# Two mixture layers that multiply only the chosen experts, with their steps placed inside the attentions

## The chip, the core and the metric

The kernel runs on one core of a Trainium2 chip. The metric is device time in microseconds (us), from one launch on that core. TensorE is called PE below, VectorE DVE, ScalarE ACT, GpSimd POOL, and SP is the engine that issues most DMAs.

## The reference

The program is a stack of four layers on `x` of shape 16 x 112 x 256 (16 batches of 112 tokens, 256 channels, float32), with a context of 16 x 375 x 256. Each layer does

```
x = x + tanh(g_xattn[l]) * attention_l(layernorm(x), ctx)
x = x + tanh(g_ffn[l])   * ffn_l(layernorm(x))
```

Attentions 0, 1 and 2 have 16 heads of width 16; attention 1 also has a mask and a clip; attention 3 has one head. The second halves are: layers 0 and 1 a mixture of 8 experts (256 to 256 channels each) of which every token uses the best two, weighted by its gates; layer 2 a set of 8 experts with fixed token blocks and a GELU; layer 3 a gated unit with FP4 quantisation. What the change touches is this:

```
gates    = softmax(x @ gate_w.T + gate_b)                # 8 per token
top2     = top_k(gates, 2)                               # layer 1: top_k of the logits, then softmax
out      = sum over the 2 chosen e of gate_e * (x @ expert_w[e] + expert_b[e])
```

## The kernel before

Tokens are handled in 4 groups of 4 batches (`G = 4`, 448 tokens). All of `x` and all of the transposed context stay in SBUF. The four compute engines run in the order in which the program emits their instructions (a manual schedule); SP's order is left to the scheduler.

The layers run one after the other. `attention(pool, layer, w)` goes over the batches b = 0..15 in a hand-written order which is software-pipelined: scores of batch b+1 and b+2 are made while batch b is weighted. In the unmasked form (layers 0 and 2) one batch on PE is: `exponentials` (L449, L461) three times, `maxima` (scores L398, whose maximum DVE takes at L414) four times, `both_keys` (L203), `values_of` (L365), `weighted` (L485) three times, `max_rows` (L434) and `output` (L522). The maxima go through POOL (`max_parts`, L422 and L425) before `max_rows`. In the masked form (layer 1) a batch is four units of four heads; a unit is scores (L398), a clip and a maximum on DVE (L548, L565), a minimum on POOL (L567), the exponential on ACT (L570), transposes (L582) and the weighting (L599). The layernorm of the next group is spread over the units of its first batch, and its last part puts three small operations, four normalisations (L269) and four additions of the output bias (L273) on POOL in one go. `one_over` (L614) on POOL and `one_over_T` (L622) on PE follow once a batch.

PSUM has two pools: three tiles of two banks each (`wide`), for scores and exponentials, and two single banks (`bank`). One of the two single banks holds the weighted sums `po` of a batch from its first `weighted` to `normalised` in the next batch, so one is left for keys, values, outputs and maxima in turn.

A mixture is a stage of its own. `Mixture.rest` goes over 16 batches, and for each of them `experts` multiplies the 112 tokens by all 8 experts, whose weights were loaded to SBUF as one tile of 2 MB. Every chosen or unchosen product is added to `x` on DVE with its gate, which is zero for the six that were not chosen:

```
for q in range(2):
    pe = wide(f"pe_{nm}_{q}")
    for n in range(2):
        c0 = (2 * q + n) * 512
        for k in range(2):
            nc.tensor.matmul(pe[:S, n, :], xT[:, k, j * S : (j + 1) * S],          # L871
                             self.ew[:, k, c0 : c0 + 512], start=(k == 0), stop=(k == 1))
    for i in range(4):
        nc.vector.scalar_tensor_tensor(xb, pe[...], gt[:, j, e : e + 1], xb, ...)   # L881
```

Between them lie, once a group, the layernorm (POOL), eight transposes (L187), the gate logits (L823) and the choice of the best two on DVE. Nothing of the next attention can start before the mixture of its first group is done, and its first steps (keys, values and queries of batch 0) follow the last mixture batch.

## Time and profile before

| what | us |
|---|---|
| median of 3 runs (1704.04 to 1705.53) | 1704.33 |
| the profiled execution | 1703.84 |
| its span, first to last instruction | 1701.6 |
| attention 0, to the last output product on PE | 0 to 323 |
| mixture 0, first transpose L187 to the keys of attention 1 | 324.1 to 471.4 |
| attention 1 (masked) | 471.4 to 868 |
| mixture 1 | 868.2 to 1014.9 |
| attention 2 | 1014.9 to 1329 |
| fixed-block experts, then layer 3 | 1329 to 1701.6 |

The times of the stages are read from the timeline of PE. A PE matrix product of float32 operands is recorded as two instructions, a transpose as one. The share of a wait is shown with what ended it; a stage in which PE is busy nearly all the time is one in which PE's work sets the time.

### The profile page before, as it was taken

The page shows a single profiled execution, that of the slowest core. Times are in us where ns is not written, and L with a number is a line of the kernel's source. Part 1 is how long each engine was busy: PE and PEld are TensorE (multiplying, and loading weights), DVE is VectorE, ACT ScalarE, POOL GpSimd, SP SyncE. Part 2 cuts the span into 40 slices and gives each one's busy share as a digit, 9 for nine tenths or more (in the row PEclk, how much of TensorE's full clock was granted, in tenths as well). Part 3 has the DMA queues.
Part 4 walks back from the last instruction along what each step waited for, and adds up shares of the span by engine and source line. Part 5 has one row for each costly group of instructions (what it writes and reads, how often), then busy time and mean ns, then how long its engine had stood idle before and what let it go on. Part 6 is the DMA issues. An engine that isn't in the chain of part 4 may idle for free.

```text
span 1701.6 us, 31829 instructions
## 1 busy us (share of the span) xinstructions
PE 1585.0 (93%) x13228; PEld 1008.9 (59%) x13228; DVE 1055.8 (62%) x1925; ACT 715.2 (42%) x1439; POOL 417.2 (25%) x856
## 2 busy tenths in 40 slices
PE   7999999999988989899899999999999899999997
PEld 3666665644456656566554444666666788666765
DVE  3565666766676766767846654565666434377775
ACT  2444444300056766677720003444444433455532
POOL 2202010212123232423310110231212334333342
PEclk8999999999999999999979998999999999999999
DMA  9000000000010000000000010000000542100000
GB/s 277 8 2 2 2 8 8 25 7 4 1 54 9 6 8 9 9 12 9 18 7 1 0 25 11 1 2 2 8 2 17 168 148 98 33 12 21 17 11 17
DMA packets 21410, 45.81 MB, mean 27 GB/s; under 512 B 4139, under 2 KB 16827, under 8 KB 18875
## 3 DMA queue, kind: packets, MB, share of 16 engines
q1 hardware_dynamic: 20835, 43.79, 8.4%
q8 instruction: 104, 1.70, 0.4%
q14 instruction: 39, 0.32, 0.1%
q10 hardware_dynamic: 432, 0.01, 0.0%
HBM read 41.95 MB, written 1.84 MB: 26 GB/s over the span
## 4 chain that ended last, share of the span: by engine, by line
PE 80%; DVE 7%; ACT 7%; POOL 4%; issue 2%; DMA 0%; SPq 0%; POOLq 0%; ACTq 0%; DVEq 0%
PE pe_m L871 13%; PE pv L365 8%; PE ps L398 8%; PE pk L203 7%; PE pe L582 6%; PE pt L449 6%; PE po L485 5%; PE py_f L966 3%; PE py L522 3%; PE ph L950 3%; PE po L599 2%; PE pq L203 2%; PE pgu_h L1289 2%; PE py L1323 2%; PE pt L461 1%
## 5 line engine op out<-in xcount | busy, mean ns | idle before, releaser
L414 DVE TENSOR_REDUCE nm<-ps 112x2 f32<-112x750 f32 x256 | 228.3, 933 | 196.2 <-PE ps L398 196.2
L871 PE MATMUL pe_m<-w_L_ffn_expert_w,xT_m 128*112 128x512 f32 x512 | 233.9, 610 | 0.0
L398 PE MATMUL ps<-kT,qm 32*112 32x375 f32 x1536 | 195.3, 528 | 20.5 <-ACT kT L329 9.6
L470 ACT ACTIVATE ex<-pt 125x896 f32<-125x896 f32 x192 | 165.6, 915 | 72.9 <-PE pt L461 72.9
L881 DVE SCALAR_TENSOR_TENSOR x<-pe_m,gt_m,x 112x256 f32<-112x256 f32 x256 | 123.7, 483 | 83.9 <-PE pe_m L871 75.2
L871 PEld LDWEIGHTS pe_m<-w_L_ffn_expert_w,xT_m 128*112 128x112 f32 x512 | 90.4, 182 | 121.8 <-issue 120.9
L570 ACT ACTIVATE sm<-sm,nmax 112x375 f32<-112x375 f32 x256 | 152.3, 599 | 8.0 <-POOL nmax L567 7.0
L582 PEld LDWEIGHTS pe<-ident,sm 112*125 112x125 f32 x768 | 105.7, 196 | 80.6 <-ACT sm L570 69.4
L582 PE MATMUL pe<-ident,sm 112*125 112x112 f32 x768 | 126.2, 294 | 26.6 <-ACT sm L570 26.1
L548 DVE SCALAR_TENSOR_TENSOR sm<-ps,up 112x750 f32<-112x750 f32 x128 | 114.0, 932 | 53.0 <-PE ps L398 52.0
L398 PEld LDWEIGHTS ps<-kT,qm 32*112 32x112 f32 x1536 | 66.3, 173 | 93.5 <-issue 39.1
L565 DVE TENSOR_REDUCE nmax<-sm 112x2 f32<-112x750 f32 x128 | 112.9, 924 | 0.0
L449 PE MATMUL pt<-qm,kT 32*125 32x224 f32 x1536 | 109.1, 381 | 3.1 <-ACT qm L355 1.7
L365 PE MATMUL pv<-w_L_xattn_wv,ctx 128*125 128x256 f32 x384 | 104.8, 413 | 0.0
L485 PE MATMUL po<-ex,vpad 125*32 125x112 f32 x3072 | 94.2, 262 | 0.7 <-ACT ex L470 0.7
L203 PE MATMUL pk<-ctx,w_L_xattn_wk 128*128 128x375 f32 x256 | 94.2, 502 | 0.0
L485 PEld LDWEIGHTS po<-ex,vpad 125*32 125x32 f32 x3072 | 70.6, 109 | 38.8 <-issue 30.4
L386 POOL TENSOR_SCALAR oT<-oT,w_L_xattn_bv 128x112 f32<-128x112 f32 x64 | 35.6, 565 | 224.0 <-DVE oT L512 173.3
L449 PEld LDWEIGHTS pt<-qm,kT 32*125 32x125 f32 x1536 | 72.9, 186 | 27.1 <-issue 17.5
L365 PEld LDWEIGHTS pv<-w_L_xattn_wv,ctx 128*125 128x125 f32 x384 | 71.6, 199 | 21.7 <-DVE x L525 7.1
L1289 PE MATMUL pgu_h<-wT,fT_f 128*112 128x352 f32 x256 | 80.1, 467 | 0.7 <-DVE x L1334 0.5
L586 ACT COPY eT<-pe 125x672 f32<-125x672 f32 x96 | 68.2, 712 | 20.3 <-PE pe L582 17.7
(254 smaller groups left out, 2513.3 us busy)
## 6 DMA issues: line engine op xcount, KB each, us to landing
w<-in_L_ffn_w_dram SPq DMA_DIRECT2D x16, 1024.0 KB, 6.2
ctx<-in_ctx_dram SPq DMA_DIRECT2D x16, 375.0 KB, 8.6
w_L_ffn_expert_w<-in_L_ffn_expert_w_dram SPq DMA_DIRECT2D x2, 2048.0 KB, 8.0
mk<-in_mask_Bx1xSxS_ik_dram SPq DMA_DIRECT2D x16, 164.1 KB, 2.3
mask<-in_mask_BxSxS_ff_dram SPq DMA_DIRECT2D x16, 164.1 KB, 2.2
x<-in_x_dram SPq DMA_DIRECT2D x4, 448.0 KB, 9.6
out_dram<-x SPq DMA_DIRECT2D x16, 112.0 KB, 1.9
w_L_ffn_w_gate_up<-in_L_ffn_w_gate_up_dram SPq DMA_DIRECT2D x1, 1408.0 KB
```

The costliest lines, as they stand in the source:

```text
L203: nc.tensor.matmul(ps[:, :n], w[:, k, c * P : (c + 1) * P], rhs[:, k, :], start=(k == 0), stop=(k == 1))
L365: nc.tensor.matmul(pv[:TC, i * D : (i + 1) * D], rhs_of(b)[:, k, t * TC : (t + 1) * TC], w["wv"][:, k, :], start=(k == 0), stop=(k == 1),)
L398: nc.tensor.matmul(ps[:S, i, :T], qms[g][rows, c, p, j * S : (j + 1) * S], kTs[b][rows, c, :], start=True, stop=True,)
L414: nc.vector.tensor_reduce(nms[b][:, cp, 2 * h : 2 * h + 2], ps[:S, :, :T], AX.X, ALU.max, negate=True)
L449: nc.tensor.matmul(pairs[r // 2][:TC, r % 2, q * 2 * S : (q + 1) * 2 * S], kTs[b][rows, c, t * TC : (t + 1) * TC], qms[g][rows, c, :, j * ...
L470: nc.scalar.activation(e[:, 2 * h : 2 * h + 2].rearrange("t r q p s -> t r (q p s)"), pairs[h][:TC, :, : 4 * S], AF.Exp)
L485: nc.tensor.matmul(po[32 * r : 32 * r + 32, (2 * c + p) * S : (2 * c + p + 1) * S], vp[:, t, 4 * c + r, 2 * p : 2 * p + 2, :], e[:, r, q, ...
L570: nc.scalar.activation(sm[:, i, :], sm[:, i, :], AF.Exp, bias=nmax[:, i : i + 1], accum_out=rss[b][:, head : head + 1])
L582: nc.tensor.transpose(pt[:TC, i, t * S : (t + 1) * S], sm[:, 2 * h + i, t * TC : (t + 1) * TC], ident[:S, :S])
L871: nc.tensor.matmul(pe[:S, n, :], xT[:, k, j * S : (j + 1) * S], self.ew[:, k, c0 : c0 + 512], start=(k == 0), stop=(k == 1),)
L881: nc.vector.scalar_tensor_tensor(xb, pe[:S, i // 2, o0 : o0 + D], gt[:, j, e : e + 1], xb, ALU.mult, ALU.add)
L1289: nc.tensor.matmul(ps[:S, n, : FI // 2], fTs[u][:, 2 * k + i, :], wT[m][:, k, n * (FI // 2) : (n + 1) * (FI // 2)], start=(k == 0), stop=( ...
```

## The change

The stage of the mixture is gone. A mixture is now three lines of small steps, each written as a generator, which are taken in turn at fixed places of the attention code. `route` normalises a group, makes gates and the best two, counts for each token its place among the tokens of its expert (products with a triangular matrix), and scatters the normalised rows with indirect DMAs from POOL to a DRAM tensor in which each expert has a region of 512 rows. It also makes a table of 14 slots: which expert, and which first row. `products` goes over these 14 slots: SP reads expert and row from the table into registers, loads that expert's weights (256 KB), its bias (128 KB, broadcast) and 128 rows of the group (128 KB); PE transposes the rows and multiplies them; DVE adds the bias; SP stores 128 rows to a second DRAM tensor. `combine` gathers for each token its two rows by indirect DMA and adds them to `x` with their gates.

`fill()` takes one step of each of the three lines, which work on different groups at a time. In an unmasked batch it is called five times: F1 after the third `maxima`, F2 after `both_keys`, F3 after the second `weighted`, F4 after the last `maxima`, F5 after the last `weighted`. In a masked batch it is called after the scores of every unit (FA) and, in the second and fourth unit, once more after the weighting of the unit before (FB). Group g of a mixture is queued when its attention has finished it, so the third and fourth group of a mixture are worked on within the next attention.

```diff
+    def products(layer, g, routed):
...
+        def read(s):
+            e = nc.sync.value_load(table[0:1, s : s + 1], min_val=0, max_val=E - 1)
+            r = regs[s] = nc.sync.value_load(table[0:1, NS + s : NS + s + 1], min_val=0, max_val=ROWS - P)
+            w = moe.tile([P, 3 * D], F32, tag="w", name=f"w_{nm}_{s}")
+            nc.sync.dma_start(w[:, : 2 * D]..., a[L + "expert_w"][:, :, bass.ds(e * D, D)])
+            nc.sync.dma_start(w[:, 2 * D :], a[L + "expert_b"][bass.ds(e, 1), :].partition_broadcast(P))
+            xg = moe.tile([P, D], F32, tag="xg", name=f"xg_{nm}_{s}")
+            nc.sync.dma_start(xg, rows_in[g][bass.ds(r, P), :])
+            loaded[s] = w, xg
+
+        read(0)
+        yield
+        read(1)
+        yield
+        for s in range(-1, NS):
+            pt = bank(f"pm_{nm}_{s}")
+            if s + 1 < NS:
+                xg = loaded[s + 1][1]
+                for k in range(2):
+                    nc.tensor.transpose(pt[:, k * P : (k + 1) * P], xg[:, k * P : (k + 1) * P], ident)
+                xgT = turnedT[s + 1] = moe.tile([P, D], F32, tag="xgT", ...)
+                nc.scalar.copy(xgT, pt[:, :D])
+            if s >= 0:
+                w, xgT = loaded.pop(s)[0], turnedT.pop(s)
+                for k in range(2):
+                    nc.tensor.matmul(pt[:, D : 2 * D], xgT[...], w[...], ...)
+                y = moe.tile([P, D], F32, tag="y", name=f"y_{nm}_{s}")
+                nc.vector.tensor_tensor(y, pt[:, D : 2 * D], w[:, 2 * D :], ALU.add)
+                nc.sync.dma_start(rows_out[g][bass.ds(regs.pop(s), P), :], y)
+                read(s + 2)
+            yield
...
+        def copy_out(j):                      # in route: four of these, one a step
+            for i in range(2):
+                nc.gpsimd.indirect_dma_start(rows_in[g], ...index[:, i, j : j + 1]..., xn[:, j, :], None)
...
+        def gather(j):                        # in combine
+            yg = got[j] = moe.tile([S, 2, D], F32, tag="yg", name=f"yg_{nm}_{j}")
+            for i in range(2):
+                nc.gpsimd.indirect_dma_start(yg[:, i, :], None, rows_out[g], ...index[:, i, j : j + 1]...)
...
+    def fill():
+        for i, make in enumerate((route, products, combine)):
+            line = lines[i]
...
+            if next(job[3], "end") == "end":
+                line.popleft()                # and on to the next line
+        next(said.get("side", iter(())), None)
...
                 maxima(b + 1, 2)
+                fill()                        # F1
                 values_of(b + 1, (0, 1))()
...
                 both_keys(b + 2)
+                fill()                        # F2
                 maxima(b + 2, 0)
                 weighted(b, 1)
+                fill()                        # F3
...
                 maxima(b + 2, 1)
-                if at == 0:
-                    norm_part(g, 2)
-                    norm_part(g, 3)
+                fill()                        # F4
                 weighted(b, 2)
+                if at == 2:
+                    bias_part(g, range(G))
+                fill()                        # F5
...
                 masked_scores(*ahead)
+                fill()                        # FA
                 turned(b, cp, 0)
                 if u:
                     weighted_masked(*units[u - 1])
+                if cp % 2:
+                    fill()                    # FB
...
-                        self.experts(g, j)
```

The rows, weights and outputs of the slots have two buffers each. In the emitted order every indirect scatter waits for the one before it, and the stores of a group wait for one another, since they write one DRAM tensor. The two DRAM tensors of each kind are cleared once by SP, 5.1 MB each, during batches 0 to 3 of attention 0.

Around this, the parts of the layernorm are placed anew: in attention 1 the four normalisations come at the end of the third batch of a group and the bias additions in two halves in the fourth, and no longer in one go. The first steps of the next attention (keys and queries of its batch 0) move into the tail of the attention before. The quantisation of the last layer's down weights, done beside mixture 0 before, becomes side steps of `fill` in attention 0, in four smaller pieces.

## The prediction

> **What bounds the kernel now.** I read the page's busy shares and its chain first, then busy time by stretch, then the timeline of one batch.

> ```profile
> PE 1585.0 (93%) x13228; PEld 1008.9 (59%) x13228; DVE 1055.8 (62%) x1925; ACT 715.2 (42%) x1439; POOL 417.2 (25%) x856
> PE 80%; DVE 7%; ACT 7%; POOL 4%; issue 2%; DMA 0%; SPq 0%; POOLq 0%; ACTq 0%; DVEq 0%
> 23.00:313.00 290.00, 275.91 (x3433) 174.14 (x3436) 176.54 (x267) 125.83 (x194) 41.49 (x115) 0.98 0.08 24
> 328.00:471.00 143.00, 138.13 (x396) 59.90 (x396) 99.03 (x265) 8.37 (x19) 22.05 (x37) 0.98 0.01 3
> 482.00:866.00 384.00, 343.88 (x3234) 233.10 (x3234) 278.02 (x404) 258.46 (x688) 124.90 (x262) 0.95 0.03 10
> 871.00:1015.00 144.00, 139.53 (x397) 61.61 (x398) 89.88 (x250) 5.07 (x12) 20.52 (x37) 0.96 0.01 2
> ```

> The rows by stretch give length, then busy PE, PE weight load, DVE, ACT, POOL, then the granted clock, DMA share and GB/s. PE is busy for 95 to 97% of attention 0 and of both mixtures, and 90% of masked attention 1; DMA moves nothing there. So removed PE work pays in full, and PE work added to an attention costs in full, and so does every wait put into PE's queue. Here is PE in one unmasked batch (start, length, what):

> ```profile
> 104.87 1.04 PE L398 MATMUL ps<-kT,qm 32*112 32x375 f32 x8
> 105.84 2.79 PE L203 MATMUL pk<-ctx,w_wk 128*128 128x375 f32 x8
> 109.51 0.90 PE L398 MATMUL ps<-kT,qm 32*112 32x375 f32 x8 [0.87 <-ACT kT L329]
> 110.34 0.97 PE L485 MATMUL po<-ex,vpad 125*32 125x112 f32 x32
> 111.25 0.37 PE L434 MATMUL pm<-identb,mparts 112*128 112x112 bf16 x4
> 111.55 1.04 PE L449 MATMUL pt<-qm,kT 32*125 32x224 f32 x16
> 112.41 0.37 PE L461 MATMUL pt<-mr,onesb 3*125 3x224 bf16 x8
> 112.71 1.13 PE L365 MATMUL pv<-w_wv,ctx 128*125 128x256 f32 x4
> 113.77 0.95 PE L398 MATMUL ps<-kT,qm 32*112 32x375 f32 x8
> 114.65 0.97 PE L485 MATMUL po<-ex,vpad 125*32 125x112 f32 x32
> ```

> F2 stands at 108.6 (in the wait for kT), F3 at 111.25, F4 at 114.65, F5 at 115.55. The reader sees how close the places are: between F2 and F3 only 1.75 us of PE work (scores .85, weighting .9), F4 to F5 .9, F3 to F4 3.4, F5 to F1 3.0 (exponentials 1.2, output .9, scores .9), F1 to F2 7.7. In a masked batch the same reading gives 1.7 from FA to FB, about 3.3 from FB to the next FA, 5 or more where there is no FB.

> **What is removed.** Mixture 0 runs from 324.05 to 471.38 and mixture 1 from 868.18 to 1014.85: 147.3 + 146.7 = 294. Two `po`, two `py` and the twelve transposes of the down weights in them stay: 5. That leaves 289. DVE loses 124 us of L881; it bounds nothing here and I count it nowhere. The second gain is the layernorm in attention 1:

> ```profile
> 507.44 2.17 POOL xn_a L269 x4
> 507.78 0.78 PE L599 MATMUL po<-eT,vpad 125*32 125x112 f32 x24
> 509.58 2.76 POOL L273 TENSOR_TENSOR x<-x,grow_a 112x256 f32<-112x256 f32 x4
> 512.28 0.39 POOL L614 COPY rx<-ri 112x256 f32<-112x256 f32 x1
> 512.73 0.64 PE L622 MATMUL pr<-ident,rx 112*128 112x112 f32 x2 [4.17 <-POOL rx L614]
> 511.80:515.20 3.40, 2.47 (x10) 2.38 (x11) 0.00 (x0) 0.89 (x2) 1.28 (x4) 0.50 0.00 0
> ```

> PE waits 4.17 for a copy that stands behind 6.5 us of POOL work, and then runs at clock 0.50 for about 3.9 us, which costs another 1.95. This happens three times (508, 605, 704). The new order puts `rx` ahead of the normalisations and halves the additions: 3 x 6.1 = 18. Together 307.

> **PE work added.** A slot has two transposes of 128 (.13 each, from L187, 8 in 1.06) and two products of 256 wide (.48 each, L365 at 1.92 for four): 1.19. There are 14 slots x 4 groups x 2 layers = 112, so 133. Note that 14 x 128 = 1792 rows is half of the 3584 of before, not a quarter: padding eats the rest. Routing costs a group 1.06 transposes, 1.65 logits (L823) and about .8 for some 18 small products: 3.5 x 8 = 28. Steps that stand where PE waits anyway are free: FA precedes L582, which waits about .4 for ACT at 43 of them, -15.

> **The wait that the change adds.** This is the main term. Rows for slot s+2 are requested after `y` of slot s, and are transposed in the very next step. The request stands on SP behind the store of y(s), 256 KB of weights and 128 KB of bias. Landing times:

> ```profile
> mask<-in_mask_BxSxS_ff_dram SPq DMA_DIRECT2D x16, 164.1 KB, 2.2
> out_dram<-x SPq DMA_DIRECT2D x16, 112.0 KB, 1.9
> w_L_xattn_wq<-in_L_xattn_wq_dram SPq DMA_DIRECT2D x3, 256.0 KB, 2.5
> ```

> [...] Three DMAs go ahead of the rows, .42 to .45 apart (b to w at 1336.81 and 1337.23, plus an address computation): 1.35. Landing is 1.9 alone. The three rows fit 1.4 + 4.5 ns per KB, so the store, weights and bias ahead of it (512 KB, 2.3 us of data) push it to 2.9 at worst; I take 2.55. R = 4.6, bounds 4.0 and 5.1. PE, in order, waits R minus the gap: F2 to F3 2.85, F3 to F4 .9 (longer gap in the batch with queries), F4 to F5 3.7, F5 to F1 1.6, F1 to F2 none: 9.0 in five, 1.8 a step. Masked: 2 x 2.9 + 2 x 1.3 in six, 1.4 a step. Slots 0 and 1 of a group are read two steps ahead, so 96 waits count; by the emitted order 41 fall in unmasked batches, 55 in masked ones: 74 + 77 = 151 (at R = 4.0 110, at 5.1 184). Behind the waiting PE stand scores, so DVE, ACT and POOL idle too, and nothing gives it back.

> **Smaller waits.** With one free PSUM bank, `pv` after F1 and `pm` after F3 wait for y: .7 each, .25 a slot, 28; F2 fills the .87 for kT in ten batches, -9. Routing takes the bank six times a group and hands it on through ACT or DVE, about 1 us each: 48. Sum 67 (25 to 85).

> POOL: the scatters of a pair wait for each other. The trace has no indirect DMA; the nearest row is the .112 MB store, 1.9. [...]

> SP: 28 register reads a group, 26 of them ahead of the first rows, five steps (18 to 20 us) before PE wants these. No register read is in the trace. [...] I take 0, range 0 to 110; there is no gain in it.

> Mask loads come on the same SP queue, but are issued a unit ahead; hidden unless SP stalls. Clearing (20 MB at the 270 GB/s of the first 23 us: 76 us) runs beside batches 0 to 3: 0, with up to 10 if a piece of the down weights lands behind it. The moved first steps of attentions 1 and 2 cost the same PE time.

> **Clock.** The row at 511.8 shows 0.50 after a wait of 4.17. [...] By the trace shorter waits also pay: about 2.3 us of transposes and logits at 353.5 were followed by 0.59. With all 34 waits above 2.8 us, 66. I take 30 (0 to 66; below nothing is excluded, 1.00 being most of the time granted).

> **Sum.** 1701.6 - 307 + 133 + 28 - 15 + 151 + 67 + 16 + 30 = 1804.6, plus the 2.2 outside the span (1703.84 - 1701.6): 1807. The profiled execution lies 0.5 below the median of 1704.33, so nothing is to be converted. All low ends: 1678; all high ends: about 2060.

> **Rivals.** (1) *Faster: the reads land soon enough.* If R is 3.0, the waits fall to .67 and .43 a step, 51, and none trips the clock: 1701.6 - 307 + 133 + 28 - 15 + 51 + 67 + 16 = 1675, with the 2.2 1677. It decides in favour from about R = 3.5 downward. [...] For: smaller waits may be less than 67. [...] (3) *The change doesn't do what it says.* Halved, not quartered, rows: taken in above. If all waits vanished, 1701.6 - 307 + 146 + 2 = 1543 would be the end; nothing in the trace lets one expect that.

> **Numbers.** Forecast .57 (1740 to 1870), rival 1 .18, rival 2 .20, a balance near zero .05. What a measurement of this kernel can tell from no change is about 0.2%. Range 1680 to 1950: it leaves out the better half of rival 1 and the upper half of rival 2.

> **What would show it.** In the profile after: PE rows of the rows' transposes (`pm_m`) with waits of 1 to 4 us put down to the DMA `xg`, some 150 in all, longest at F5 and F3; PE's busy share falling below 90%; dips of the clock there; a pair of scatters of about 4 us on POOL; batches of about 34 us instead of 17.9 where products run. Waits for `xg` below 50 in all, or first slots waiting over 10 us, would make the prediction wrong.

## The result, and the profile after

The changed kernel takes 2225.27 us (median of 4 runs, 2218.96 to 2232.72) where the kernel before takes 1704.18 on the same chip: a ratio of 1.306, 95% interval 1.3014 to 1.3106. The profiled execution took 2228.51 us, its span 2226.8. "Slower" was right, and the wait that the rows put on PE was right in place and, partly by luck, in size, but the loss is 521 us where 103 were forecast, far outside the range. One term, the clock, was too small by a factor of eight, and one wait was not in the sum at all.

First the page after: busy shares, the rows of the 40 slices for PE and for its granted clock, and the chain that ended last.

```profile
PE 1733.4 (78%) x13404; PEld 1164.5 (52%) x13404; DVE 1011.9 (45%) x1965; ACT 754.3 (34%) x1550; POOL 546.8 (25%) x1003
PE   7898777677676766766766766777779999999998
PEclk7999786877867866786787677768679999999999
PE 39%; ACT 8%; DVE 7%; issue 5%; DMA 5%; POOL 3%; SPq 2%; POOLq 0%; DVEq 0%; ACTq 0%
```

PE's share falls from 93% to 78% and no other engine's share rises. PE is no longer the whole chain: 39% after 80%. From slice 5 to slice 30, which is where mixture steps stand, the busy digit is 6 or 7 and the clock digit mostly 6 to 8; from slice 31 on both are 9. So two things are lost together: time in which PE does nothing, and speed in the time in which it works. The same by stretch (length, busy PE, weight load, DVE, ACT, POOL, granted clock, DMA share, GB/s):

```profile
313.00:800.00 487.00, 346.76 (x2576) 228.14 (x2577) 193.48 (x411) 138.06 (x312) 109.66 (x183) 0.74 0.24 67
800.00:1300.00 500.00, 349.93 (x2207) 236.36 (x2207) 201.55 (x386) 166.93 (x446) 116.35 (x203) 0.74 0.21 61
1300.00:1715.00 415.00, 304.25 (x2533) 193.46 (x2532) 170.89 (x335) 121.86 (x248) 97.97 (x175) 0.78 0.21 59
1715.00:1820.00 105.00, 100.84 (x1311) 65.00 (x1312) 62.15 (x95) 49.19 (x79) 18.21 (x47) 1.00 0.01 4
```

In 313 to 1715 PE sits idle for 401 us. What it does in the rest, it does at 0.74 to 0.78: 346.76 x 0.26 + 349.93 x 0.26 + 304.25 x 0.22 = 248 us that the same work would not have taken at full clock. In the fourth row, in attention 2 behind the mixture's last products, the clock is 1.00 again. This gives a way to split every span of this study: PE's idle time, the clock loss (busy time times one minus the granted clock, summed over stretches of 1.7 us), and what is left, which is PE's work at full clock. It is taken from one profiled execution of each kernel.

| kernel | span | PE idle | clock loss | work at full clock |
|---|---|---|---|---|
| before | 1701.6 | 116.5 | 46.5 | 1538.5 |
| after | 2226.8 | 493.3 | 297.4 | 1436.1 |
| difference | +525 | +377 | +251 | -102 |

The work went down as it should. Idle time and clock loss took it back six times over. Where PE waits, in the view of waits (who waits for whom, us in all, times, longest):

```profile
PE pm_m L1112 <- DMA xg_m<-rows_in: 167.4, 52, 5.9
PE pm_m L1118 <- ACT xgT_m L1114: 105.3, 104, 6.1
PE pe L622 <- ACT sm L610: 53.0, 22, 10.2
```

The first line is the wait that the prediction put at 151. The second was not in it. The third is twice the 26.1 that `pe` waited for `sm` before. Here are two slots in an unmasked batch, on PE's timeline:

```profile
437.25 0.66 PE L1112 MATMUL pm_m<-ident,xg_m 128*128 128x128 f32 x2 [5.01 <-DMA xg_m<-rows_in]
438.43 2.08 PE L1118 MATMUL pm_m<-w_m,xgT_m 128*128 128x256 f32 x4 [0.52 <-ACT xgT_m L1114]
...
446.87 0.41 PE L1112 MATMUL pm_m<-ident,xg_m 128*128 128x128 f32 x2 [2.50 <-DMA xg_m<-rows_in]
447.80 1.13 PE L1118 MATMUL pm_m<-w_m,xgT_m 128*128 128x256 f32 x4 [0.52 <-ACT xgT_m L1114]
```

Read each pair of lines. PE waits 5.01 us for the rows of the next slot, transposes them, and then waits again, .52 us, before the products. These products are of the slot before, whose transposed rows were ready a step ago; yet they start right after ACT has copied the rows that were transposed just now. So the pipelining by one slot, which the code writes down, does not happen. And the products after the 5.01 take 2.08 us, those of the next pair of lines 1.13, for the same four instructions: that is the clock, 0.50 in the first place and 1.00 in the second.

```profile
425.06:428.47 3.41, 1.05 (x10) 0.23 (x4) 1.78 (x2) 0.95 (x3) 0.00 (x0) 1.00 0.37 105
428.47:431.89 3.42, 3.17 (x32) 2.35 (x36) 0.43 (x1) 0.19 (x1) 0.00 (x0) 0.50 0.02 5
431.89:435.30 3.41, 0.34 (x12) 0.10 (x4) 0.00 (x0) 0.45 (x1) 0.00 (x0) 1.00 0.49 133
435.30:438.71 3.41, 0.94 (x3) 0.57 (x4) 0.00 (x0) 0.37 (x1) 0.00 (x0) 0.50 0.22 62
438.71:442.13 3.42, 3.42 (x24) 2.39 (x28) 0.42 (x1) 0.00 (x0) 0.00 (x0) 0.50 0.06 20
442.13:445.54 3.41, 2.23 (x24) 1.05 (x16) 1.64 (x3) 1.73 (x2) 0.00 (x0) 1.00 0.51 138
445.54:448.95 3.41, 1.54 (x6) 0.88 (x6) 2.63 (x9) 0.37 (x1) 0.47 (x2) 1.00 0.12 35
448.95:452.37 3.42, 2.87 (x7) 2.32 (x8) 3.27 (x7) 0.00 (x0) 1.04 (x1) 0.50 0.34 104
452.37:455.78 3.41, 3.41 (x67) 2.25 (x65) 0.57 (x2) 2.35 (x4) 0.00 (x0) 1.00 0.46 95
```

Each of the four windows in which PE was busy for less than half (1.05, 0.34, 0.94, 1.54) is followed by one at 0.50. Of those at 0.50, each of the three that PE nearly filled (3.17, 3.42, 2.87) is followed by one at 1.00. The windows of all thirteen traces from 25 us on, counted by PE's busy share and by the clock of the next window:

| clock of the window | PE busy in it | next window at 0.50 |
|---|---|---|
| 1.00 | below 45% | 268 of 274 |
| 1.00 | 45 to 60% | 142 of 298 |
| 1.00 | above 60% | 78 of 5291 |
| 0.50 | below 80% | 276 of 276 |
| 0.50 | 80 to 95% | 215 of 261 |
| 0.50 | above 95% | 65 of 504 |

So short waits add up within a window: the one from 445.54 holds 1.33 us of the wait of 2.50 and the .52 after it, and the next is at 0.50. At half clock, a window in which PE was idle for more than a fifth was followed by another at half clock in 276 of 276 cases. The changed kernel has 80 stretches at half clock, 9.7 us long on average; the kernel before has 17, of 6.4.

### The profile page after: what moved, and what is told of

It is laid out like the page before. It is cut to its first block, busy times and chain, and to the rows that moved or that the text cites. A ratio compares the mean times of both kernels' runs of the same rounds, so it can differ in the third digit from the quotient of the medians.

```text
span 2226.8 us, 35033 instructions
## 1 busy us (share of the span) xinstructions
PE 1733.4 (78%) x13404; PEld 1164.5 (52%) x13404; DVE 1011.9 (45%) x1965; ACT 754.3 (34%) x1550; POOL 546.8 (25%) x1003
## 4 chain that ended last, share of the span: by engine, by line
PE 39%; ACT 8%; DVE 7%; issue 5%; DMA 5%; POOL 3%; SPq 2%; POOLq 0%; DVEq 0%; ACTq 0%
PE pv L405 5%; PE pm_m L1118 4%; DMA xg_m<-rows_in 4%; PE pk L230 4%; PE pe L622 3%; ACT sm L610 3%; PE ps L438 3%; PE py_f L1269 2%; PE ph L1253 2%; PE pt L489 2%; PE pgu_h L1599 2%; PE py L562 2%; PE po L525 1%; PE py L1633 1%; PE po L639 1%
## 5 line engine op out<-in xcount | busy, mean ns | idle before, releaser
L1118 PE MATMUL pm_m<-w_m,xgT_m 128*128 128x256 f32 x448 | 193.1, 574 | 107.8 <-ACT xgT_m L1114 105.3
L1127 DVE TENSOR_TENSOR y_m<-pm_m,w_m 128x256 f32<-128x256 f32 x112 | 47.5, 425 | 424.4 <-PE pm_m L1118 246.4
L1112 PE MATMUL pm_m<-ident,xg_m 128*128 128x128 f32 x208 | 55.2, 357 | 187.1 <-DMA xg_m<-rows_in 167.4
L1118 PEld LDWEIGHTS pm_m<-w_m,xgT_m 128*128 128x128 f32 x448 | 110.1, 272 | 158.1 <-ACT xgT_m L1114 137.8
L622 PE MATMUL pe<-ident,sm 112*125 112x112 f32 x768 | 146.4, 339 | 53.1 <-ACT sm L610 53.0
L622 PEld LDWEIGHTS pe<-ident,sm 112*125 112x125 f32 x768 | 141.4, 252 | 87.8 <-ACT sm L610 67.0
L405 PE MATMUL pv<-w_L_xattn_wv,ctx 128*125 128x256 f32 x384 | 132.3, 495 | 18.4 <-ACT y L568 7.9
L1112 PEld LDWEIGHTS pm_m<-ident,xg_m 128*128 128x128 f32 x208 | 25.9, 170 | 227.8 <-issue 184.2
L1114 ACT COPY xgT_m<-pm_m 128x256 f32<-128x256 f32 x104 | 38.2, 367 | 297.5 <-PE pm_m L1112 297.5
L607 POOL TENSOR_SCALAR nmax<-nmax 112x2 f32<-112x2 f32 x128 | 26.8, 219 | 297.3 <-DVE nmax L605 295.8
## 6 DMA issues: line engine op xcount, KB each, us to landing
w_m<-in_L_ffn_expert_w_dram SPq DMA_DIRECT2D x112, 256.0 KB, 3.2
```

What stands on the lines that cost most here:

```text
L405: nc.tensor.matmul(pv[:TC, i * D : (i + 1) * D], rhs_of(b)[:, k, t * TC : (t + 1) * TC], w["wv"][:, k, :], start=(k == 0), stop=(k == 1),)
L622: nc.tensor.transpose(pt[:TC, i, t * S : (t + 1) * S], sm[:, 2 * h + i, t * TC : (t + 1) * TC], ident[:S, :S])
L1112: nc.tensor.transpose(pt[:, k * P : (k + 1) * P], xg[:, k * P : (k + 1) * P], ident)
L1118: nc.tensor.matmul(pt[:, D : 2 * D], xgT[:, k * P : (k + 1) * P], w[:, k * D : (k + 1) * D], start=(k == 0), stop=(k == 1), skip_group_che ...
```

## The experiments

Theory A: the loss is made of waits on PE, of which rows, the same-step copy and the one free PSUM bank are the three large ones, and the clock falls because of the waits, so that time comes back at more than the wait's own length when they go. Theory B, the rival: the clock falls because of the kind of work (small float32 products and transposes between other work, at a higher DMA load), or the steps cost by being there, so that taking waits away brings back their own length at most. All ratios are against the kernel before, run beside the variant on the same chip (its medians lie between 1702.15 and 1704.88 us); line numbers of variants move by a few.

**Rows requested a step earlier.** Three row buffers instead of two, one buffer for `y`; the request for the rows leaves ahead of weights and bias.

```diff
+        def rows(s):
...
+            xgs[s] = moe.tile([P, D], F32, tag="xg", ..., bufs=AHEAD)      # AHEAD = 3
+            nc.sync.dma_start(xgs[s], rows_in[g][bass.ds(regs[s], P), :])
...
                 nc.sync.dma_start(rows_out[g][bass.ds(regs.pop(s), P), :], y)
+                rows(s + AHEAD)
                 read(s + 2)
```

> The rows of a slot are requested one step earlier (three row buffers, one output buffer in place of two). Theory A: the waits in PE's queue trip the TensorE clock, so the 170 us of waits for the rows go and take with them their share of the lost clock (251 us more PE time than before the change; 170 of 377 us of added idle time, so about 110): about 1940 us, granted clock near 0.88. Theory B: the clock is low because of the kind of work in the steps, whatever the waits: only the 170 go, about 2055 us, clock still 0.83.

Measured: 1978.46 us (1964.55 to 1986.3), ratio 1.162 [1.1595, 1.1645]. The waits of PE in this kernel:

```profile
PE pm_m L1127 <- ACT xgT_m L1123: 120.4, 104, 6.1
PE pe L623 <- ACT sm L611: 47.1, 21, 9.1
```

Of the waits for `xg` 1.5 us are left. 167 us of wait taken away brought 247 us of time, which is nearer to theory A (1940) than to B (2055). In the profiled execution, 14 us faster than the median, idle time fell by 147 and clock loss by 131 (166.0 left); the granted clock was 0.899. The same-step wait is now by far the largest, and larger than before.

**Products ahead of transposes.** In a step, the two products of slot s are emitted before the two transposes of slot s+1; nothing else.

```diff
             pt = bank(f"pm_{nm}_{s}")
+            if s >= 0:
+                ... products of slot s
             if s + 1 < NS:
                 ... transposes of slot s+1, nc.scalar.copy(xgT, pt[:, :D])
-            if s >= 0:
-                ... products of slot s
```

> In a step the two products of slot s come ahead of the transposes of slot s+1. The wait of every product for the copy made in the same step (105 us in 104 steps) goes, and the rows have about 0.9 us more to land (some 50 us of their 170). Theory A: 155 us and some 100 of clock, about 1970 us. Theory B: about 2070 us.

Measured: 2048.72 us (2044.82 to 2049.57), ratio 1.2011 [1.1991, 1.2031].

```profile
PE pm_m L1123 <- DMA xg_m<-rows_in: 144.3, 46, 6.8
```

The products' wait for ACT's copy is gone, the one for the rows stays: it fell by 23 us and not by 50, and the waits for `y` rose from 24.8 to 56.8 us. What was left of the gain is 177 us, 89 idle and 92 clock. The time is nearer to theory B (2070) than to A (1970), since fewer waits went than expected; that half of what came back is clock (0.874 granted, after 0.825) speaks for A.

**Both.** The two edits above together.

> Both edits: rows one step earlier, products ahead of transposes. Theory A: 275 us of waits and about 180 of clock go: about 1770 us, clock 0.92 or more. Theory B: about 1950 us, clock still near 0.83. If the waits only move to the weights or to the one free PSUM bank: above 2000 us, with new waits for w or y in place.

Measured: 1836.69 us (1831.94 to 1841.4), ratio 1.0782 [1.0764, 1.08]; 281.2 us idle, clock loss 114.3. Each alone brought 247 and 177, together 389, somewhat less than their sum of 424. The time lies between theory A (1770) and B (1950); the granted clock of 0.924 is what A expected. Two waits stand out now. One is for the exponential of the masked attention. The other is 81.6 us for DVE's `y` in 68 places, of which these are the largest; the users of the single free bank wait for it.

```profile
PE pe L623 <- ACT sm L611: 47.0, 24, 9.1
PE pv L406 <- DVE y_m L1137: 21.3, 9, 4.7
PE pk L231 <- DVE y_m L1137: 20.2, 16, 2.3
PE py L563 <- DVE y_m L1137: 16.3, 15, 1.8
```

**The changed kernel with useless work put into the wait.** Sixteen transposes of the identity stand ahead of the row transposes in every step with a next slot; their result is overwritten at once. The data, the order of all else and what waits for what are those of the changed kernel.

```diff
                 xg = loaded[s + 1][1]
+                for k in range(16):
+                    nc.tensor.transpose(pt[:, :P], ident, ident)
                 for k in range(2):
```

> The kernel after, with 16 more transposes of the identity (results overwritten) ahead of the wait for the rows in each of 112 steps: 2.1 us each at full clock, 235 us of added PE work. Theory A: it keeps PE active in place of waiting, the clock rises to 0.9 or more, and the time stays the same or falls (2050 to 2230 us). Theory B: the half of it that doesn't fall into waits adds to the time: 2330 us or more, clock no higher than 0.83.

Measured: 2192.83 us (2187 to 2207.73), ratio 1.2876 [1.2817, 1.2934]. PE was given 216 us of work at full clock (1652.2 against 1436.1), and the kernel became 32 us faster. Idle time fell by 124, and so did the clock loss, by 126. The stretch that had 0.74 above, in this kernel:

```profile
313.00:800.00 487.00, 381.74 (x3165) 270.32 (x3166) 193.59 (x411) 138.26 (x312) 109.22 (x183) 0.86 0.23 67
```

The added work, float32 transposes, is of a kind that theory B blames, and the DMA load is the same 67 GB/s; the clock rose from 0.74 to 0.86, and to 0.909 over the whole span. Theory B has fallen. In this kernel the clock is lost where PE stands still, not by what PE does: with 216 us more work and 124 us less idle time the loss went from 297.4 to 171.3 us.

**Products in a PSUM tile of their own.** On the kernel with earlier rows, in the order of the change (transposes first), the products go to a tile of the three wide ones and no longer to the other half of the bank of the transposes. This asks why a product waits for a copy that it does not read.

```diff
             pt = bank(f"pm_{nm}_{s}")
+            pw = wide(f"pw_{nm}_{s}") if s >= 0 else None
...
-                        pt[:, D : 2 * D],
+                        pw[:, 1, :D],
```

> The kernel with earlier rows (order as changed: transposes of slot s+1, then products of slot s), with the products in a tile of their own from the three wide ones. Theory D: the products wait for ACT's copy of the same step only because both use one PSUM tile. Then the 120 us of waits of PE for xgT in 104 places fall to below 15, and with the clock's share the time from 1978 to about 1800 (1978 - 110 - 60). Rival: the wait comes from the order alone (the step's copy stands ahead of the product on the way of the data, or ACT's counter is waited for as a whole): it stays at 100 or more, and the time above 1930.

Measured: 1736.46 us (1729.54 to 1744.76), ratio 1.0193 [1.0149, 1.0238]. The 120.4 us of waits in 104 places have become this:

```profile
PE pk L231 <- ACT xgT_m L1124: 1.4, 3, 0.5
```

So the wait came from what the two share and not from the order: the copy reads one half, the product writes the other, and the program as built has the product wait. The time fell further than the 1800 expected; the waits for `y`, which no longer holds the free bank, fell too, from 35.8 us to 4.9. The tile is also one bank here, so this run alone doesn't tell which of the two it is; the next one does.

**The bank.** On the kernel with both edits, transposes and products use the two halves of a wide tile (two banks) instead of the one free bank.

```diff
-            pt = bank(f"pm_{nm}_{s}")
+            pw = wide(f"pm_{nm}_{s}")
...                                              # products to pw[:, 1, :D], transposes to pw[:, 0, ...]
```

> Both earlier edits, and a step takes one of the three wide PSUM tiles in place of the one free single bank. If the waits of keys, values, outputs and maxima for y (75 us with both edits) come from the bank, they go, with some 35 us of clock: about 1730 us. If scores and exponentials then wait for a wide tile instead, nothing is won: 1820 us or more, with new waits of ps or pt for DVE.

Measured: 1719.28 us (1716.34 to 1723.24), ratio 1.0104 [1.0082, 1.0125]. Waits for `y` fell from 81.6 us in 68 places to 7.1 in 8; idle time fell by 77 and clock loss by 36, and 115 us came back ((1.0782 - 1.0104) x 1702). Of the 521 us lost, 17 are left. In this kernel the halves lie in two banks of one tile, and DVE's `y`, which reads one, still waits for ACT's copy, which reads the other:

```profile
DVE y_m L1137 <- ACT xgT_m L1134: 84.3, 62, 5.7
```

Nothing else in the code joins these two. So in the program as built the tile ties its users together, even across banks. Transposes and products in two separate wide tiles were not tried.

**One scatter a step.** `copy_out` sends one indirect DMA per step instead of a pair; once on the kernel with both edits, once on the kernel with wide tiles.

```diff
-        def copy_out(j):
-            for i in range(2):
+        def copy_out(j, i):
...
+        for j in range(1, G):
+            for i in range(2):
+                copy_out(j, i)
+                yield
```

> Both earlier edits (rows one step earlier, products first), and one scatter a step in place of two, so that no scatter waits on POOL for the one just issued. If blocked POOL is what makes the transposes of attention 1 wait for the exponential (47 us with both edits, 27 before the change), 20 us of waits and about 10 of clock go: about 1805 us. If POOL's blocks are hidden: 1837 us, the waits unchanged.

> All of it: rows earlier, products first, wide tiles, one scatter a step. If all waits named are independent and each takes its share of the clock along: about 1700 us, level with the kernel before. If something else holds the steps (weights, SP, the single store buffer): 1760 us or more.

Measured: 1827.8 us (1824.1 to 1833.37), ratio 1.0743 [1.0716, 1.077] on the first, where 30 us were expected and about 9 came, little more than the noise (the interval of the kernel with both edits begins at 1.0764); on the second 1693.34 us (1688.46 to 1703.85), ratio 0.9957 [0.9944, 0.9969], 26 less than with pairs. The same edit is worth more once the other waits are gone. What POOL's queue still does shows in the worst place of this second kernel; these are lines of the timelines of POOL and then PE:

```profile
928.90 1.09 POOL L1049 DMA_INDIRECT rows_in<-xn_m,index_m  x1 [0.18 <-issue]
930.29 0.98 POOL L1152 DMA_INDIRECT yg_m<-rows_out,index_m  x1 [0.30 <-issue]
931.57 0.94 POOL L1152 DMA_INDIRECT yg_m<-rows_out,index_m  x1 [0.30 <-issue]
932.54 0.43 POOL L608 TENSOR_SCALAR nmax<-nmax 112x2 f32<-112x2 f32 x2
...
933.58 0.76 PE L623 MATMUL pe<-ident,sm 112*125 112x112 f32 x2 [8.72 <-ACT sm L611]
```

PE waits 8.72 us for an exponential, the exponential for a minimum of .43 us, and the minimum stands behind one scatter and two gathers on POOL (and four normalisations and two steps of the mask ahead of these).

**The minimum on DVE.** This edit moves that minimum to DVE, in the last kernel; and, as a control, in the kernel before with the normalisation moved (next paragraph), where POOL has no indirect DMA.

```diff
-                nc.gpsimd.tensor_scalar(part, part, 100.0, None, ALU.min)
+                nc.vector.tensor_scalar(part, part, 100.0, None, ALU.min)
```

> The one-scatter kernel with wide tiles, with the minimum of the masked attention (L608) moved from POOL to DVE. Theory C: what is left of the loss is POOL's queue: the minimum stands behind scatters and gathers, ACT waits 33.6 us for it in 15 places and PE 43 us for ACT (sm 32.1, nmax 5.3, issue 5.2). Then these waits fall to about 10 and the clock loss of 69 by some 15: about 1693 - 33 - 15 = 1645, below the kernel with the moved normalisation alone (1675). Rival: the waits are set by ACT's and DVE's own queues (y waits 53.7 us for its store on DVE), and the minimum then stands behind y instead: 1685 to 1695.

> The kernel before with the moved normalisation, and the same minimum on DVE. Here no indirect DMA stands on POOL. Theory C: little changes, 1675 less at most 5. If it falls by as much as the kernel with the mixtures in the attentions, the minimum's place on POOL cost by itself and not through the indirect DMAs.

Measured: 1660.55 us (1659.1 to 1664.2), ratio 0.9755 [0.9742, 0.9768], and for the control 1678.37 us (1673.75 to 1685.64), ratio 0.9859 [0.9837, 0.9881], no different from without the edit. So the minimum's place on POOL costs nothing by itself; the gain of 33 needs what the mixtures put on POOL beside the attentions. In the kernel before this edit that is 125 us of indirect DMAs and 31 us of their layernorm; the runs do not part the two. In the first:

```profile
PE pe L623 <- ACT sm L611: 17.2, 19, 3.7
PE pe L623 <- DVE sm L589: 12.8, 13, 2.8
```

The first line was 32.1 us before the edit, its longest 8.7. The second was 1.4 us and takes part of it back, which may be why 33 came and not the 48 expected. This is the fastest kernel of the study, faster than the one before and than the change. It also speaks once more against theory B:

```profile
PE 1487.8 (90%) x13404; PEld 1028.8 (62%) x13404; DVE 1028.2 (62%) x2093; ACT 751.6 (45%) x1550; POOL 522.3 (32%) x875
DMA packets 127263, 150.38 MB, mean 91 GB/s; under 512 B 13496, under 2 KB 118328, under 8 KB 125048
```

PE has the same 13404 instructions as in the changed kernel, and the DMAs move the same 150.4 MB in less time, yet the granted clock is 0.958 and not 0.825.

**The layernorm of attention 1 alone.** The kernel before, with mixtures as they were; only the normalisations and bias additions of attention 1 are split as the change splits them. They stand here in the first and second batch of a group, where the change has them in the third and fourth.

```diff
...                                              # the one block of before becomes rows_part and bias_part
+                if at == 0 and cp == 3:
+                    rows_part(g)
+                if at == 1 and cp in (0, 1):
+                    bias_part(g, range(2 * cp, 2 * cp + 2))
```

> The kernel before, with one part of the change alone: in attention 1 the four normalisations come behind the copy rx, and the bias additions in two halves in the next batch. If the prediction's term is right, the three waits of 4.2 us and the half clock behind each go: 18 us less, 1686 us. If the waits only move to the minimum on POOL: 1700 us or more.

Measured: 1675.07 us (1673.9 to 1685.29), ratio 0.9859 [0.9832, 0.9885]. Nearly the same work as the masked stretch of before, 482 to 866 (3219 of 3234 PE instructions), in 356 us at full clock:

```profile
482.00:838.00 356.00, 328.56 (x3219) 222.00 (x3219) 275.94 (x402) 256.82 (x685) 124.80 (x262) 1.00 0.04 10
```

All kernels by the split used above:

| kernel | median | PE idle | clock loss | work at full clock |
|---|---|---|---|---|
| layernorm alone, minimum on DVE | 1678.37 | 100.5 | 35.8 | 1538.5 |
| layernorm alone | 1675.07 | 103.6 | 28.2 | 1539.9 |
| before | 1704.18 | 116.5 | 46.5 | 1538.5 |
| wide, one scatter, minimum on DVE | 1660.55 | 169.6 | 59.6 | 1428.2 |
| wide, one scatter | 1693.34 | 190.0 | 69.3 | 1431.7 |
| wide | 1719.28 | 204.2 | 78.6 | 1431.8 |
| earlier rows, products apart | 1736.46 | 215.9 | 98.2 | 1423.8 |
| both, one scatter | 1827.8 | 275.0 | 114.0 | 1433.8 |
| both | 1836.69 | 281.2 | 114.3 | 1434.7 |
| earlier rows | 1978.46 | 346.4 | 166.0 | 1450.4 |
| after, with useless work | 2192.83 | 369.7 | 171.3 | 1652.2 |
| products first | 2048.72 | 404.6 | 205.0 | 1437.5 |
| after | 2225.27 | 493.3 | 297.4 | 1436.1 |

The nine mixture kernels without useless work have the same products to do, and their last column runs from 1423.8 to 1450.4. So the split is good to some 15 us.

## Why the prediction went wrong, point by point

- *What is removed and added in work*: right. Over the two mixtures the rows of before give 138.13 x 0.98 + 139.53 x 0.96 = 269 us of PE work at full clock, and 133 + 28 were to come back: -108. Measured -102. (The pieces of a slot add to 1.22 and not 1.19 us, which is 4 us more in all.)
- *The layernorm in attention 1, -18*: right in cause, small in size. Done alone it is worth 27.1 (1702.15 to 1675.07; by the interval of the ratio 20 to 29). The waits were read rightly: 12.5 us in three places, all gone, and idle time fell by 12.9. The clock was not: its loss fell by 18.3 where 5.9 was taken. This is the error of the clock term below, in small.
- *The wait for the rows, +151*: right in place and cause, and 167.4 in size, but the size is partly luck. Two of R's three pieces were too small: landing took 3.3 us where 2.55 was taken, and the three DMAs ahead of the request with their addresses 2.0 to 2.4 (449.47 to 451.48 in one step) where 1.35 was taken. Only `y` was quicker: no run shows the .7 that R has for it, and in the changed kernel it took .54 (440.51 to 441.05). That makes R about 6, above its bound of 5.1, and by the prediction's own gaps the wait would have been some 250 us (an estimate). It fell in 52 places instead of 96, 3.2 us long on average; in the others the rows were there in time, so the steps stood further apart than was read from the kernel before.
- *The wait that was not in the sum*: the prediction read the pipelining by one slot from the code and costed the copy between transposes and products at nothing. The two share one PSUM tile, and each of 104 steps waits about 1 us, 105 in all; the edit that takes the wait away alone was worth 177 us. This is a step that failed: nothing in the profile of before spoke for cover, and what was to be asked was where the product's output lies, not only what it reads.
- *Bank waits, +67*: right in mechanism. Its part for `y`, 28, was 24.8 us after the change; its part for routing, 48, was about half of that in the list of waits. The price of the bank was hidden by the larger waits: when these had gone, `y` was waited for 81.6 us, and the bank was worth 115 us.
- *POOL, +16, 0 to 60*: right in cause, at the high end of the range. No run of before shows the time of a scatter on which the 16 rests; in the changed kernel a pair took 3.8 us (696.84 to 700.68), with 2.5 us from issue to landing, and the wait for `sm` grew by 27 us. One scatter a step was worth 9 us among other waits and 26 without them; with the minimum's 33 on top, POOL's queue costs 59 in the mended kernel.
- *Register reads on SP at nothing*: right that they are hidden, though no row of before shows a read, so that the 0 and its range to 110 were the author's guess. In the changed kernel the 26 reads ahead of the first rows took 14.8 us, .57 each (the load itself .27); the first slots of all groups together waited 2.2 us.
- *The clock, +30, 0 to 66*: this is the term that broke the sum. It was 251. The step that failed: only single waits above 2.8 us were priced, each with about 2 us of loss at half clock after it, and 66 was called the high end; no run shows the 30, a choice between 0 and 66. The runs show another price. The clock of a window went with PE's busy share in the 3.413 us before it (half clock after 268 of 274 windows below 45%, after 78 of 5291 above 60%), so waits below 2.8 us count too; and the stretches at half clock of the changed kernel last 9.7 us on average, not 3.9. Long gaps alone price it too low: the changed kernel has 41 idle gaps of PE of 3.4 us or more; at the prediction's 1.95 us each they make some 80 us (an estimate), against 297 measured. With earlier rows there are 11, some 21 us, against 166. The row of before that the prediction quoted, 0.59 after some 2.3 us of transposes and logits, pointed to the loss and was used only for a bound.
- *Rival 1* ("the reads land soon enough", 1677): its premise was made true by the earlier rows, and the kernel took 1978; its sum has nothing for the clock, and 166 us of clock loss were left. Rows that land in time were not enough by themselves; the rows had to land, the same-step wait had to go and the bank to be set free to come to 1719.
- *Rival 2*, that SP's register reads and POOL's scatter pairs hold PE up, is not what happened. The register reads stayed hidden, 2.2 us of waits in all, and the wait for `sm` grew by 27 us, which leaves most of the loss to other causes.
- *Rival 3's end, 1543*, where all waits vanish, was not reached: the best kernel has 53 us more idle time and 13 more clock loss than before, against 110 of work saved, and stands at 1660.55.

Together, in the terms of the split: the forecast of +103 us comes to about -108 of work, +195 of idle time and +16 of clock loss, once the idle time and clock loss in its -307 are put where they belong. Measured are -102, +377 and +251. Of the 423 us between the two sums, 235 are the clock, 105 the wait that was not in the sum, 27 the wait for `sm`, 16 the rows, and the rest smaller waits and work. The signs that were named beforehand did come: 167 us of waits for `xg`, PE at 78%, a scatter pair of 3.8 us. They tested the rows' wait, not the sum.

## What to carry to other kernels

Split a span into PE's work at full clock, its idle time and its clock loss before pricing a change, and charge every microsecond that PE is left idle at 1.5 to 2: in these runs 377 us more idle time came with 251 us of clock loss, and each microsecond of idle time taken away brought 0.5 to 1 us of clock loss back with it (131 for 147, 92 for 89, 36 for 77). Look for the half clock where PE's busy share in windows of 3.413 us falls to 60% and below: in these traces it followed after 410 of 572 such windows at full clock, and after 78 of 5291 above 60%. The software pipeline written in the code was not one in the traces where two of its stages shared a buffer: one PSUM tile cost 120.4 us of waits with earlier rows, and the only free bank 81.6 with both edits; so ask for each step who else touches the tile that it writes. And look for the small part of a large change: moving four normalisations and their bias additions, a side edit here, is worth 27 us alone, next to the 43 us that the whole change brings with the edits above.

## What the runs showed of the hardware that was not expected

The clock loss grows faster than the idle time: 28 us at 104 idle, 69 at 190, 114 at 281, 166 at 346, 205 at 405 and 297 at 493, over kernels whose waits differ in kind, and 171 at 370 for the one with 216 us of useless work. So in these kernels idle time was not free of charge even where it looked like slack, and work put into a wait made the changed kernel faster, by 32 us. The table of windows goes with this: at full clock 268 of 274 windows less than 45% busy were followed by half clock, and at half clock all 276 windows less than 80% busy were. A likely reason for the bend, argued and not tested, is that with more waits more of them fall into windows that are already at half clock and keep the clock there: the stretches at half clock last 6.0 to 7.2 us on average in the kernels with up to 346 us of idle time, 8.1 at 405 and 9.7 at 493 (6.5 with the useless work). What decides between 45 and 60% (142 of 298) these runs do not settle. Also open is how far below 1660.55 the mended kernel could come: with a second buffer for `y`, or weights requested earlier, which were not tried.
